# Attention scores in four query groups instead of two halves, PSUM as one tile, and padded TensorE steps

## The chip, the cores and the metric

The kernel runs on one core of a Trainium2 chip. The metric is the device time of one execution in microseconds (us). TensorE is called PE below, VectorE DVE, ScalarE ACT, GpSimd POOL, and SyncE, which issues most DMAs, SP.

## What is computed

One transformer layer with cross-attention, all in float32. `x` (queries) and `ctx` (keys and values) are 128 x 128 x 256: 128 sequences of 128 tokens. There are 16 heads of 16 channels and a hidden layer of 1024.

```
q = x @ Wq + bq ; k = ctx @ Wk + bk ; v = ctx @ Wv + bv        # 16 heads of 16
scores = q @ k^T / 4 ; keep only keys j < i ; attn = softmax(scores)
attn[row 0] = 0
y   = layer_norm(x + (attn @ v) @ Wo + bo, ln1)
out = layer_norm(y + relu(y @ W1 + b1) @ W2 + b2, ln2)
```

Query i sees only the keys before it. Half of each 128 x 128 score matrix is therefore never used.

## The kernel before

The kernel handles the sequences in pairs: 64 steps, one for each pair p. The order of instructions on every engine is written out by hand. The first steps (`third`, `fourth`, `fifth`, and what stands ahead of them) are special; from p = 5 on all are made by `step(p)`, and `behind` ends the pipeline. Several pairs are in work at the same time. `step(p)` issues in this order on PE:

- `weigh(p - 2)`: softmax weights times values into `pc` (PSUM bank 7), 96 matmul passes in 32-column strips of the array (L471, L481)
- `scores_both(p)`: the scores into `pss` (L364)
- `queries(p + 1)` into `pq` (bank 4), `attention_out(p - 2)` into `po` (bank 5), `keys(p + 1)` into `pk` (bank 0), `values(p)` into `pv` (bank 1)
- `second_by_seven(p - 4)`: the second FFN product into `py`, `pz` (banks 6 and 7, L780), as seven half-size products
- `hidden(p - 3)`: the first FFN product into `ph` (banks 2, 3, 4, 0, L687)

A float32 matmul shows up in the trace as two passes, each with a weight load (LDWEIGHTS, row PEld) and a MATMUL (row PE); a shape "32*64 32x128" means 32 rows by 64 columns of the array in use and 128 columns streamed. A transpose on PE is one pass.

The scores are made in two halves of queries. The low half (queries 0 to 63) gets 64 keys, the high half 128 keys. The two sequences of the pair sit in the two halves of the 128 partitions, and all 16 heads of a query lie in one partition. The high half goes to banks 0 to 3, one bank for each strip of four heads, the low half to banks 4 to 7. The array is used as 4 x 2 tiles of 32 rows and 64 columns: one row strip for each strip of heads, one column half for each sequence. `scores_both` alternates between the strips `two` and `one`, so that the banks that are needed soonest are read soonest.

DVE then adds the mask (`mask`, L378; `mask_high`, L729), takes maxima (L733, L740), ACT makes the exponentials head by head (`exponential_by_head`, L748), DVE sums them (`sums`, L409), POOL divides (L411), DVE transposes 32 x 32 blocks (`turn`, into `tb`, L424) and 16 DMAs on SP bring the blocks to the partitions of the keys (`bring`, into `pT`, L439). `weigh` uses `pT` two steps later. `sm`, `tb` and `pT` rotate through the four buffers of the pool tag `wide`. Each PSUM bank is a tile of its own (`at_bank`).

The first matmul of `pq` takes bank 4 and waits until DVE has read the low scores of that bank; that of `pk` takes bank 0 and waits for ACT; that of `pc` takes bank 7 and waits for `sum_of_seven` on DVE.

Of the kernel before, what the change touches and what calls it, by code (L numbers as in the profile page):

```python
# [13 lines left out]
P = 128  # L14
# [5 lines left out]
def tile_cross_attention_block(  # L20
# [53 lines left out]
    states = {}  # L74

# [96 lines left out]

    one = const.tile([1, P], F32, tag="one", name="one")
# [36 lines left out]
    def at_bank(i, name):  # L210
        return psum.tile([P, 512], F32, tag=f"b{i}", name=name)
# [101 lines left out]
    def wide(name):  # L313
        return soft.tile([P, NS * (H + HH) * 32], F32, tag="wide", name=name, bufs=4)
# [32 lines left out]
    def scores_both(p):  # L347

        st = states[p]
        for hi in range(2):  # L350
            st["sps", hi] = [
                at_bank(r if hi else (6, 7, 4, 5)[r], f"pss{hi}_{p}_{r}") for r in range(NS)
            ]
            room(p, hi)
        one, two = (0, 1), (2, 3)
        for strips, hi, m in (
            (two, 0, 0), (one, 1, 0), (two, 0, 1), (one, 1, 1),
            (two, 1, 0), (two, 1, 1), (one, 0, 0), (one, 0, 1),
        ):
            n = P if hi else HP  # L360
            for s in range(2):
                for r in strips:
                    strip, first = slice(32 * r, 32 * r + 32), s * P
                    nc.tensor.matmul(  # L364
                        st["sps", hi][r][
                            s * HP : (s + 1) * HP, m * 2 * n : (m + 1) * 2 * n
                        ].rearrange("p (e j) -> p e j", e=2),
                        st["qT"][strip, m, first + hi * HP : first + hi * HP + HP],
                        st["kT"][strip, m, :, first : first + n],
                        start=True, stop=True,  # L370
                    )

# [45 lines left out]
    def turn(p, hi, t):  # L418

        st = states[p]  # L420
        if "tb" not in st:
            st["tb"] = wide(f"tb_{p}").rearrange("p (j n) -> p j n", j=NS)
        at = (t if hi else 2) * 256
        nc.vector.transpose(  # L424
            st["tb"][:, :, at : at + 256].rearrange("p j (n a) -> p n j a", a=32),
            st["sm", hi].rearrange("p h j -> p (h j)")[:, t * 1024 : (t + 1) * 1024].rearrange(
                "p (n j a) -> p n j a", j=NS, a=32
            ),
        )

    def bring(p, queue, which):

        st = states[p]
        if "pT" not in st:
            pT = st["pT whole"] = wide(f"pT_{p}").rearrange("p (i n) -> p i n", i=NS)
            st["pT"] = pT.rearrange("p i (n a) -> p i n a", a=32)
        for u in which:
            i, j = u // NS, u % NS
            queue.dma_start(  # L439
                st["pT whole"][32 * j : 32 * j + 32, i, :], st["tb"][32 * i : 32 * i + 32, j, :]  # L440
            )

    def turn_on_pe(p, hi, ts):

        st = states[p]
        sm = st["sm", hi].rearrange("p h j -> p (h j)")
        if "pT" not in st:
            pT = wide(f"pT_{p}").rearrange("p (i n) -> p i n", i=NS)
            st["pT"] = pT.rearrange("p i (n a) -> p i n a", a=32)
        for t in ts:  # L450
            pt = bank(f"ptp{hi}_{p}_{t}")
            for i in range(4):
                at = (4 * t + i) * P
                nc.tensor.transpose(pt[:, i * P : (i + 1) * P], sm[:, at : at + P], ident)
            n = 4 * t if hi else H + 4 * t
            nc.scalar.copy(
                st["pT"][:, :, n : n + 4, :].rearrange("p i n a -> p n i a"),
                pt.rearrange("p (n i a) -> p n i a", i=NS, a=32),
            )

    def weigh(p):
# [3 lines left out]
        pc = at_bank(7, f"pc_{p}") if p > 1 else bank(f"pc_{p}")  # L465

        for m in range(KC):
            for s in range(2):
                at = (m * 2 + s) * P
                for j in range(NS):  # L470
# [3 lines left out]
                        pT[:, 2 * s : 2 * s + 2, H + 2 * j + m, :],  # L474
                        start=True, stop=True,
                    )
            for s in range(2):
                at = (m * 2 + s) * P
                for e in range(2):
                    for j in range(NS):  # L480
# [5 lines left out]
                            pT[:, 2 * s : 2 * s + 2, 4 * j + 2 * m + e, :],  # L486
# [189 lines left out]
    def hidden(p, fs, between=None):  # L676
# [3 lines left out]
        for f in fs[::2]:  # L680
# [4 lines left out]
            for i in range(2):  # L685
                for k in range(KC):
# [4 lines left out]
                    )  # L691
            for i in range(2):
# [31 lines left out]
    def mask_high(p, rs):  # L724

        st = states[p]
        for r in rs:
            ps = st["sps", 1][r].rearrange("p (n j) -> p n j", j=P)
            nc.vector.tensor_tensor(  # L729
                ps[:, :, HP:], ps[:, :, HP:], neg[:, 1, None, :].to_broadcast([P, 4, HP]), ALU.add  # L730
            )
        for r in rs:
            nc.vector.tensor_reduce(  # L733
                st["nmx", 1][:, 4 * r : 4 * r + 4],
                st["sps", 1][r].rearrange("p (n j) -> p n j", j=P), AX.X, ALU.max, negate=True,
            )

    def low_maximum(p):
        st = states[p]
        nc.vector.tensor_reduce(st["nmx", 0], st["sm", 0], AX.X, ALU.max, negate=True)  # L740

    def exponential_by_head(p, hi, heads):

        st = states[p]
        sm, nmx = st["sm", hi], st["nmx", hi]
        for h in heads:
            src = st["sps", 1][h // 4][:, h % 4 * P : h % 4 * P + P] if hi else sm[:, h, :]
            nc.scalar.activation(sm[:, h, :], src, AF.Exp, bias=nmx[:, h : h + 1], scale=1.0)  # L748
# [22 lines left out]
    def second_by_seven(p):  # L771
# [6 lines left out]
        def product(out, left, right):  # L778
            for k in range(FC // 2):
                nc.tensor.matmul(  # L780
                    out, left(k), right(k), start=(k == 0), stop=(k == FC // 2 - 1)
                )

# [6 lines left out]
        product(py[:, :P], raw(0, 0), weights(0, 0))  # L790
        product(pz[:, :P], raw(1, 0), weights(1, 0))
        product(pz[:, 2 * P : 3 * P], raw(1, 1), lambda k: wt[:, 3, k])
        product(py[:, 3 * P :], lambda k: hs[:, 0, k], lambda k: wt[:, 0, k])
        product(py[:, 2 * P : 3 * P], lambda k: hs[:, 2, k], lambda k: wt[:, 2, k])
        product(py[:, P : 2 * P], lambda k: hs[:, 1, k], lambda k: wt[:, 1, k])
        product(pz[:, P : 2 * P], lambda k: hs[:, 3, k], weights(1, 1))
# [159 lines left out]
    nc.gpsimd.tensor_tensor(be1b_r, be1_r, b2_r, ALU.add)  # L956
    values(2)
# [11 lines left out]
    def low_scores(p):  # L969
        scores(p, 0)  # L970
        mask(p, 0, A)
        mask(p, 0, B)
        maximum(p, 0, ALL)
# [3 lines left out]
    def third():  # L977
        p = 2
        scores(p, 1)
        mask(p, 1, A)  # L980
        maximum(p, 1, ONE)
# [5 lines left out]
        mask(p, 1, B)  # L987
        maximum(p, 1, TWO)
        exponential(p, 1, ONE)
# [7 lines left out]
        sums(p, 1, ONE)  # L997
        exponential(p, 1, TWO)
# [3 lines left out]
        exponential(p, 0, ALL)  # L1002
        sums(p, 1, TWO)
# [3 lines left out]
        sums(p, 0, ALL)  # L1007
        add_bo(2)
        turn(p, 1, 0)
        turn(p, 1, 1)  # L1010
        attention_out(p - 1)
        attention_sum(p - 1)
        turn(p, 0, 0)
        bring(p, nc.sync, EVERY[:8])
# [11 lines left out]
        hidden(0, range(3 * FC // 4, FC), lambda f: bring(p, nc.scalar, EVERY[8:]))  # L1026
# [3 lines left out]
    def fourth():  # L1030
        p = 3
        load_ahead(p)
        scores(p, 1)
        mask(p, 1, A)
        maximum(p, 1, ONE)
        second(0, 0)
        mask(p, 1, B)
        maximum(p, 1, TWO)
        exponential(p, 1, ONE)
        second(0, 1)  # L1040
        tokens(p + 2, "c")
        sums(p, 1, ONE)
        exponential(p, 1, TWO)
        second_sum(0)
        sums(p, 1, TWO)
        weigh(p - 1)
        context(p - 1)
        scores(p, 0)
# [3 lines left out]
        mask(p, 0, A)  # L1052
        mask(p, 0, B)
        maximum(p, 0, ALL)
        exponential(p, 0, ALL)
        turn(p, 1, 0)
        turn(p, 1, 1)
# [4 lines left out]
        sums(p, 0, ALL)  # L1062
# [4 lines left out]
        turn(p, 0, 0)  # L1067
        bring(p, nc.sync, LATE_FIRST)
        stats(0, states[0]["t2"], 2)
        scale_and_shift(0)  # L1070
        norm2(0)

    def fifth():
# [3 lines left out]
        mask(p, 0, B)  # L1077
        mask(p, 1, A)
        maximum(p, 1, ONE)
        queries(p + 1)  # L1080
        mask(p, 1, B)
        maximum(p, 1, TWO)
        exponential(p, 1, ONE)
        mask(p, 0, A)
        maximum(p, 0, ALL)
        keys(p + 1)
        exponential(p, 1, TWO)
        values(p)
        values_out(p)
        sums(p, 1, ONE)  # L1090
        exponential(p, 0, ALL)
        sums(p, 1, TWO)
        sums(p, 0, ALL)
# [5 lines left out]
        turn(p, 1, 0)  # L1099
        turn(p, 1, 1)  # L1100
        turn(p, 0, 0)
        bring(p, nc.sync, LATE_FIRST)
        hidden(2, range(FC // 2))

    ONES, TWOS = range(HH), range(HH, H)
    POOL_ALONE = (nc.gpsimd, nc.gpsimd)

    def step(p):
        last = p == NP - 1
        weigh(p - 2)  # L1110
        context(p - 2)
        scores_both(p)
        if p > 6:
            combine_hidden(p - 4, POOL_ALONE)
        if p == 5:
            second_sum(1)
            finish(0)
            store(0)
        add_bo(p - 1)
        load_ahead(p)  # L1120
        mask(p, 0, B)
        mask_high(p, A)
        exponential_by_head(p, 1, ONES)
        mask_high(p, B)
        exponential_by_head(p, 1, TWOS)
        mask(p, 0, A)
        low_maximum(p)
        if p > 5:
            exponential_by_head(p, 0, range(H))
# [9 lines left out]
        if p == 5:  # L1139
            exponential_by_head(p, 0, range(H))  # L1140
# [4 lines left out]
        sums(p, 1, ONE)  # L1145
        sums(p, 1, TWO)
        sums(p, 0, ALL)
# [12 lines left out]
        turn(p, 1, 0)  # L1160
        if p > 6:
            sum_of_seven(p - 4)
        turn(p, 1, 1)
        turn(p, 0, 0)
        bring(p, nc.sync, LATE_FIRST)
# [106 lines left out]
```

## Time and profile before

| what | value |
|---|---|
| time, median of 3 runs (lowest, highest) | 1553.75 us (1552.18, 1554.89) |
| the profiled execution: its time, its span | 1555.99 us, 1554.0 us |
| mean granted PE clock | 0.995 of full speed |
| busy: PE, DVE, POOL, ACT | 1521.2, 1327.8, 1265.7, 1120.5 us |
| passes on PE | 17926 |
| DMA moved | 204.21 MB, mean 131 GB/s |

The span runs from the first to the last instruction; the profiled execution takes 1.99 us more than its span and lies 2.24 us above the median. Ends of matmuls are modelled, so that starts are the better guide: the time of a stage is read from its first start to the first start of the stage after it.

### The profile page before, as it was taken

How to read it: one execution, taken by the hardware profiler on the slowest of the kernel's cores; microseconds unless marked ns; L12 is line 12 of the kernel's file. 1: busy time of each engine (PE TensorE's matmuls, PEld its weight loads, DVE VectorE, ACT ScalarE, POOL GpSimd, SP SyncE). 2: the span in 40 equal slices, each digit the busy share in tenths (PEclk: the TensorE clock that was granted, in tenths of full speed). 3: DMA queues.
4: the chain of work that ended last, by engine and by line, in shares of the span. 5: the costliest groups of instructions: out<-in, count | busy, mean ns of one | idle time of the engine just before them, and what ended most of it. 6: DMA issues, size and time to landing. Idle time of an engine off the chain costs nothing.

```text
span 1554.0 us, 47426 instructions
## 1 busy us (share of the span) xinstructions
PE 1521.2 (98%) x17926; PEld 1363.3 (88%) x17926; DVE 1327.8 (85%) x2490; ACT 1120.5 (72%) x3391; POOL 1265.7 (81%) x1290
## 2 busy tenths in 40 slices
PE   8997999999999999999999999999999999999998
PEld 7786989989899889899899899899898899899887
DVE  7987889888889889889889889889889889888854
ACT  5656778777778768778778778678778677777742
POOL 6875888887888888888888888888888888888874
PEclk9999999999999999999999999999999999999999
DMA  8355655555566556556556566556565566554431
GB/s 196 83 120 120 143 134 134 136 132 136 137 138 142 131 134 140 138 134 144 121 138 146 132 140 138 128 136 148 131 139 130 131 138 149 133 136 120 107 91 48
DMA packets 415283, 204.21 MB, mean 131 GB/s; under 512 B 282448, under 2 KB 383056, under 8 KB 415056
## 3 DMA queue, kind: packets, MB, share of 16 engines
q1 hardware_dynamic: 413152, 200.13, 55.7%
q8 instruction: 142, 2.33, 0.7%
q10 hardware_dynamic: 1904, 1.06, 0.3%
q14 instruction: 85, 0.70, 0.1%
HBM read 70.26 MB, written 33.29 MB: 67 GB/s over the span
## 4 chain that ended last, share of the span: by engine, by line
PE 92%; DVE 3%; POOL 3%; issue 1%; ACT 1%; DMA 0%; POOLq 0%; DVEq 0%
PE ph L687 27%; PE py L780 13%; PE pz L780 10%; PE pq L257 8%; PE po L500 7%; PE pv L289 7%; PE pk L257 7%; PE pss L364 6%; PE pc L481 3%; PE pc L471 2%; POOL sm L411 1%; PE py L705 0%; DVE tb L424 0%; DVE sm L378 0%; POOL sd L521 0%
## 5 line engine op out<-in xcount | busy, mean ns | idle before, releaser
L687 PE MATMUL ph<-x1T,w 128*128 128x256 f32 x2048 | 454.0, 379 | 3.0 <-ACT kT L279 3.0
L687 PEld LDWEIGHTS ph<-x1T,w 128*128 128x128 f32 x2048 | 384.6, 190 | 53.9 <-ACT kT L279 3.4
L411 POOL TENSOR_TENSOR sm<-sm,rs 128x1024 f32<-128x1024 f32 x192 | 359.3, 1898 | 7.1 <-ACT hT L693 4.5
L693 ACT ACTIVATE hT<-ph,b1e_c 128x256 f32<-128x256 f32 x504 | 209.8, 468 | 188.3 <-PE ph L687 181.3
L748 ACT ACTIVATE sm<-pss,nmx 128x128 f32<-128x128 f32 x944 | 249.8, 415 | 132.4 <-DVE nmx L733 72.5
L748 ACT ACTIVATE sm<-sm,nmx 128x64 f32<-128x64 f32 x944 | 231.9, 334 | 5.1
L409 DVE TENSOR_REDUCE su<-sm 128x8 f32<-128x1024 f32 (+1 forms) x192 | 225.8, 1176 | 9.4 <-ACT sm L748 5.6
L378 DVE TENSOR_TENSOR sm<-pss,neg 128x256 f32<-128x256 f32 (+1 forms) x276 | 108.0, 433 | 133.0 <-PE pss L364 125.2
L424 DVE STREAM_TRANSPOSE tb<-sm 128x1024 f32<-128x1024 f32 x186 | 220.7, 1213 | 0.0
L520 POOL TENSOR_SCALAR ve<-mv 128x2 f32<-128x2 f32 x127 | 29.7, 234 | 212.4 <-DVE mv L514 212.0
L780 PE MATMUL py<-wt,hS 128*128 128x128 f32 x1440 | 172.0, 276 | 2.9 <-POOL hS L767 2.9
L780 PEld LDWEIGHTS py<-wt,hS 128*128 128x128 f32 x1440 | 166.4, 192 | 3.5 <-POOL hS L767 3.5
L733 DVE TENSOR_REDUCE nmx<-pss 128x4 f32<-128x512 f32 x236 | 150.5, 678 | 0.0
L257 PE MATMUL pq<-xT,wq 128*128 128x256 f32 x504 | 127.3, 396 | 4.9 <-DVE sm L378 4.9
L279 ACT ACTIVATE kT<-pk,bkh,half 128x256 f32<-128x256 f32 x252 | 120.3, 558 | 4.0 <-PE pk L257 4.0
L289 PE MATMUL pv<-wv,cT 128*128 128x256 f32 x512 | 121.1, 379 | 1.6 <-ACT sm L748 1.6
L500 PE MATMUL po<-wo,cxT 128*128 128x256 f32 x512 | 122.4, 382 | 0.0
L257 PE MATMUL pk<-cT,wk 128*128 128x256 f32 x504 | 119.2, 379 | 0.0
L257 PEld LDWEIGHTS pq<-xT,wq 128*128 128x128 f32 x504 | 91.7, 192 | 25.8 <-issue 9.4
L289 PEld LDWEIGHTS pv<-wv,cT 128*128 128x128 f32 x512 | 97.1, 190 | 15.1 <-ACT sm L748 2.0
L500 PEld LDWEIGHTS po<-wo,cxT 128*128 128x128 f32 x512 | 98.0, 192 | 14.0 <-ACT cxT L493 0.3
L257 PEld LDWEIGHTS pk<-cT,wk 128*128 128x128 f32 x504 | 95.7, 190 | 13.1 <-issue 0.2
(131 smaller groups left out, 2973.3 us busy)
## 6 DMA issues: line engine op xcount, KB each, us to landing
pT<-tb SPq DMA_DIRECT2D x984, 96.0 KB
x1t<-tbx SPq DMA_DIRECT2D x252, 64.0 KB
x1T<-x1t SPq DMA_DIRECT2D x63, 256.0 KB
out_dram<-t SPq DMA_DIRECT2D x63, 256.0 KB
xb<-in_x_dram SPq DMA_DIRECT2D x124, 128.0 KB
cb<-in_ctx_dram SPq DMA_DIRECT2D x124, 128.0 KB
x<-in_x_dram SPq DMA_DIRECT2D x31, 512.0 KB
w<-in_L_xattn_W_dram SPq DMA_DIRECT2D x2, 1024.0 KB
```

Source lines behind the costliest of these rows:

```text
L257: nc.tensor.matmul(ps[:, m * TP : (m + 1) * TP], w[:, k, m * P : (m + 1) * P], src[:, k, :], start=(k == 0), stop=(k == KC - 1),)
L279: nc.scalar.activation(st["kT"][:, m, e, :], pk[:, m * TP : (m + 1) * TP], AF.Identity, bias=bkh[:, m, e : e + 1], scale=half[:, e : e + 1],)
L289: nc.tensor.matmul(pv[:, s * D : (s + 1) * D], st["cT"][:, k, s * P : (s + 1) * P], wv[:, k, :], start=(k == 0), stop=(k == KC - 1),)
L409: nc.vector.tensor_reduce(su, sm[:, part, :], AX.X, ALU.add)
L411: nc.gpsimd.tensor_tensor(sm[:, part, :], sm[:, part, :], rs[:, :, None].to_broadcast([P, part.stop - part.start, n]), ALU.mult,)
L424: nc.vector.transpose(st["tb"][:, :, at : at + 256].rearrange("p j (n a) -> p n j a", a=32), st["sm", hi].rearrange("p h j -> p (h j)")[:, ...
L500: nc.tensor.matmul(po[:, s * D : (s + 1) * D], cxT[:, k, s, :], wo[:, k, :], start=(k == 0), stop=(k == KC - 1),)
L687: nc.tensor.matmul(ph[:, i * TP : (i + 1) * TP].rearrange("p (s i a) -> p s i a", s=2, a=32), w1[:, k, (f + i) * P : (f + i + 1) * P], st[ ...
L693: nc.scalar.activation(st["hT"][:, f + i, :], ph[:, i * TP : (i + 1) * TP], AF.Relu, bias=(b1e_c if p else b1_c)[:, f + i : f + i + 1], sc ...
L733: nc.vector.tensor_reduce(st["nmx", 1][:, 4 * r : 4 * r + 4], st["sps", 1][r].rearrange("p (n j) -> p n j", j=P), AX.X, ALU.max, negate=True,)
L748: nc.scalar.activation(sm[:, h, :], src, AF.Exp, bias=nmx[:, h : h + 1], scale=1.0)
L780: nc.tensor.matmul(out, left(k), right(k), start=(k == 0), stop=(k == FC // 2 - 1))
```

## The change

Scores, softmax and the way to `pT` work in four groups g of 32 queries, with 32, 64, 96 and 128 keys. A partition now holds a query of one sequence for one half of the heads: 2 sequences x 2 head halves x 32 queries make the 128 partitions, with 8 heads in each. The array is used as 4 x 4 tiles of 32 x 32 (row strip of heads, column strip c of sequence and head half). A step has 64 score matmuls (128 passes) in place of 32 (64 passes).

- All of PSUM is one tile `banks`, and `at_bank` returns a slice of it. Groups 3 and 2 share banks 0 to 3, groups 1 and 0 banks 4 to 7.
- `sm`, `nmx`, `su`, `rs` hold four groups; a partition has 2560 weights in place of 3072. `wide` has two buffers: `sm` always takes one and `tb` the other. `pT` is two constant tiles, zeroed once by `clear` where no DMA writes. The 16 DMAs stay, two of four shapes shorter.
- The masks of the last 32 keys of each group come from one 128 x 128 tile `diag`; `mask_high` adds them for groups 3 and 2 in one instruction for two banks.
- `empty(n)` issues n empty instructions (`nop`) on PE: 10 or 11 after each of the seven products of `second_by_seven`, and 3 or 4 after each matmul of `hidden` for p < 3.
- At p = 5, `second_sum(1)` stands before the scores.

The core of the diff:

```diff
+    banks = psum.tile([P, 8, 512], F32, tag="banks", name="banks")
     def at_bank(i, name):
-        return psum.tile([P, 512], F32, tag=f"b{i}", name=name)
+        return banks[:, i, :]
+
+    def empty(n):
+        for _ in range(n):
+            nc.tensor.nop(hint="pad", nofuse=True)
...
+    LENGTH = (32, 64, 96, 128)
+    WITHIN = (0, 32, 0, 96)
+    HI, LO = (3, 2), (1, 0)
+    def first_bank(p, g):
+        return 4 if p > 3 and g < 2 else 0
+    def place(g, r):
+        return r if g > 1 else (r + 2) % 4
...
+    def group_scores(p, g, strips=range(NS)):
+        st = states[p]
+        n = LENGTH[g]
+        for m in range(KC):
             for s in range(2):
+                c = 2 * s + m
                 for r in strips:
                     strip, first = slice(32 * r, 32 * r + 32), s * P
+                    out = banks[32 * c : 32 * c + 32, first_bank(p, g) + place(g, r)]
                     nc.tensor.matmul(
...
-                        st["qT"][strip, m, first + hi * HP : first + hi * HP + HP],
+                        out.rearrange("p (e x) -> p e x", e=2)[:, :, WITHIN[g] : WITHIN[g] + n],
+                        st["qT"][strip, m, first + 32 * g : first + 32 * g + 32],
                         st["kT"][strip, m, :, first : first + n],
                         start=True, stop=True,
                     )
+    def scores_both(p):
+        one, two = (0, 1), (2, 3)
+        for strips, g in (
+            (two, 1), (one, 3), (two, 0), (one, 2),
+            (two, 3), (one, 1), (two, 2), (one, 0),
+        ):
+            group_scores(p, g, strips)
...
+    def masked(p, g, at=slice(0, 4)):
+        n = LENGTH[g]
+        heads = slice(2 * at.start, 2 * at.stop)
+        nc.vector.tensor_tensor(
+            weights(p, g)[:, heads], in_banks(p, g, at),
+            diag[:, None, P - n :].to_broadcast([P, 2 * (at.stop - at.start), n]), ALU.add,
+        )
...
-        def product(out, left, right):
+        def product(out, left, right, after):
             for k in range(FC // 2):
                 nc.tensor.matmul(
                     out, left(k), right(k), start=(k == 0), stop=(k == FC // 2 - 1)
                 )
+                empty(after // (FC // 2) + (after % (FC // 2) > k))
...
     def step(p):
...
-        mask(p, 0, B)
-        mask_high(p, A)
-        exponential_by_head(p, 1, ONES)
-        mask_high(p, B)
-        exponential_by_head(p, 1, TWOS)
-        mask(p, 0, A)
-        low_maximum(p)
+        for g in LO:
+            masked(p, g, FORE)
+        mask_high(p, FORE)
+        exponential_by_head(p, HI, ONES)
+        mask_high(p, REAR)
+        exponential_by_head(p, HI, TWOS)
+        for g in LO:
+            masked(p, g, REAR)
+        for g in LO:
+            largest(p, g)
```

`FORE` and `REAR` are the first and the last two banks of a group of four. The order of the other calls in `step` is as before.

More of the change, by code (lines that the diff above doesn't have):

```diff
@@ L345, in scores @@
         room(p, hi)
-    def scores_both(p):
-        st = states[p]
[L350 to L360, printed above, removed]
+    pTs = []
@@ L373, in mask, with brought @@
+    def brought(p, queue, which):
+        st = states[p]
+        st["pT"] = pTs[p % 2]
+        pT = pTs[p % 2].rearrange("p i t n a -> p i (t n a)")
+        for u in which:
+            i, j = u // NS, u % NS
+            first = (0, 128, 0, 384)[j]
+            queue.dma_start(
+                pT[32 * j : 32 * j + 32, i, first:], st["tb"][32 * i : 32 * i + 32, j, first:]
+            )
     def mask(p, hi, rs):
@@ L978, in third @@
         p = 2
-        scores(p, 1)
-        mask(p, 1, A)
-        maximum(p, 1, ONE)
+        for g in HI:
+            group_scores(p, g)
+        masked(p, 3)
+        shifted(p, 3)
         turn_x1_on_pe(0)
@@ L1051, in fourth @@
         queries(p + 1)
[L1052 to L1057, printed above, removed]
+        for g in LO:
+            masked(p, g)
+        for g in LO:
+            shifted(p, g)
+        for g in LO:
+            powers(p, g)
+        turned(p, 3)
+        turned(p, 2)
         attention_out(p - 1)
@@ L1066, in fourth @@
         turn_x1(p - 1)
[L1067 to L1068 removed]
+        for g in LO:
+            turned(p, g)
+        brought(p, nc.sync, LATE_FIRST)
         stats(0, states[0]["t2"], 2)
```

284 lines of the change are left out of this document (173 added, 111 removed).

## The prediction

> **What bounds the kernel now.** I read the page's busy times and its chain first, then the table by stretches for one step in the middle, then the timeline of PE for that step, and last PE's idle times.
>
> ```profile
> PE 1521.2 (98%) x17926; PEld 1363.3 (88%) x17926; DVE 1327.8 (85%) x2490; ACT 1120.5 (72%) x3391; POOL 1265.7 (81%) x1290
> 319.56:342.85 23.29, 23.29 (x281) 21.07 (x280) 20.65 (x40) 17.74 (x55) 19.63 (x20) 1.00 0.56 125
> 342.85:367.85 25.00, 23.67 (x281) 21.20 (x280) 20.85 (x40) 17.85 (x55) 20.87 (x24) 1.00 0.62 146
> ```
>
> The second and third rows are two steps that follow each other, each from the start of its `weigh` to the next one's: length, then busy time of PE, PEld, DVE, ACT and POOL, the granted clock, DMA. In the first PE is busy all 23.29 us, at full clock, and DVE is the next with 20.65. So in a plain step only what PE itself does counts. The second step is 1.71 us longer, and PE is idle for 1.33 us in it. How a plain step is made up, from the timeline of PE (start, length, line, count):
>
> ```profile
> 812.74 0.43 PE L471 MATMUL pc<-pT,vd 128*32 128x64 f32 x16
> 814.22 1.63 PE L364 MATMUL pss<-kT,qT 32*64 32x128 f32 x64
> 815.78 1.99 PE L257 MATMUL pq<-xT,wq 128*128 128x256 f32 x8
> 817.61 1.89 PE L500 MATMUL po<-wo,cxT 128*128 128x256 f32 x8
> 822.79 1.05 PE L780 MATMUL py<-w,hT 128*128 128x128 f32 x8
> 823.68 1.06 PE L780 MATMUL pz<-w,hT 128*128 128x128 f32 x8
> 829.04 7.07 PE L687 MATMUL ph<-x1T,w 128*128 128x256 f32 x32
> 836.04 0.43 PE L471 MATMUL pc<-pT,vd 128*32 128x64 f32 x16
> ```
>
> From start to start: `weigh` 1.48, scores 1.56, and every other pass at the rate of its columns: eight passes of 128 columns in 0.89 (111 ns each), 32 of 256 in 7.00 (219, the drain included). The 96 passes of `pc`, in four column strips side by side, take 15.4 ns each, so 62 ns for each strip's pass of 64 columns. A pass thus costs some 0.82 ns a column and 6 ns; TensorE streams without a break.
>
> The third piece is what makes some steps longer. The weight loads of the scores that found nothing to do:
>
> ```profile
> 129.90 0.42 PEld L364 LDWEIGHTS pss<-kT,qT 32*64 32x64 f32 x21 [1.22 <-issue]
> 347.23 0.19 PEld L364 LDWEIGHTS pss<-kT,qT 32*64 32x64 f32 x3 [1.58 <-issue]
> 557.85 0.19 PEld L364 LDWEIGHTS pss<-kT,qT 32*64 32x64 f32 x3 [0.87 <-issue]
> 768.82 0.19 PEld L364 LDWEIGHTS pss<-kT,qT 32*64 32x64 f32 x4 [1.16 <-issue]
> 979.17 0.19 PEld L364 LDWEIGHTS pss<-kT,qT 32*64 32x64 f32 x4 [0.58 <-issue]
> 1190.08 0.20 PEld L364 LDWEIGHTS pss<-kT,qT 32*64 32x64 f32 x5 [1.19 <-issue]
> 1400.42 0.20 PEld L364 LDWEIGHTS pss<-kT,qT 32*64 32x64 f32 x5 [0.61 <-issue]
> q8 instruction: 142, 2.33, 0.7%
> ```
>
> "issue" means that PE waited for nothing that the profile shows. From the second row on they come every 210.6 us, nine steps. The last row is the queue that brings PE's instructions: 142 packets of 16.4 KB, one for some 256 of the 36,400 instructions. A step of the built program has 569 PE instructions; nine make 5121, 20 blocks and 1 instruction over, so every ninth step lies alike to the blocks. Counted in the trace, all seven stalls fall on number 193 of a block. So PE waits for its own instructions: `weigh` and the scores issue 320 in 3 us, a block change falls 57 behind the start of `weigh`, and the next, 256 on, comes before its block is there. The six stalls behind the first sum to 5.99 us; the step shown lost 0.13 more than its idle row, so the six cost 6.8 us.
>
> **The sum, part by part.**
>
> *Place of the blocks.* With the empty instructions the changed program has exactly 768 PE instructions, three blocks, from one `weigh` to the next, from step 7 to the end of `step`. `weigh` always starts on number 225, and the scores end 450 later. Changes lie 32 ahead of `weigh`, 224 behind its start (in the scores) and 480 behind it (in `po`). The first is passed in `hidden`, long before. The second is passed some 1.7 us into the stretch, and its follower is needed at 1.48 + 1.56 + 1.83 (`pq`) + seven passes of `po` (1.5) = 6.4 us, 4.7 us later. In the stalled step the change was passed at about 0.4 us and PE went on at 347.23 - 342.85 = 4.4 us, so a block takes up to 4.0. The margin is 0.7 us, and a stall there would be small. Value: -6.8; between -6.8 and -3.
>
> The Trainium skill ("Runtime: NRT & Kernel Launch", Instruction fetch mechanics) states blocks of 16 KiB or 256 instructions, as here, and that crossing a block is mostly hidden; by that this term would be nothing and the time 1552.5. The stalls above, 0.58 to 1.58 us, speak against it in this stretch.
>
> *The empty instructions themselves.* 74 in a step of `second_by_seven`. The trace has none; the nearest thing that only PE's sequencer handles is a wait:
>
> ```profile
> L364 PEldq EVENT_SEMAPHORE  x119: 51/51/51, 84.5 to 1468.9; - x119
> ```
>
> A half-size matmul streams for 2 x 111 = 223 ns and has 2.6 of them behind it: 2.6 x 51 = 135 ns of issue. They hide behind the stream, and `hidden` behind them (64 instructions in 7 us) gives the lead back. The three or four behind each matmul of the first three `hidden` have 2 x 216 ns and hide too. The cover is gone above 84 ns each. If they held the array they would cost 74 x 51 ns = 3.8 us a step. Value 0.
>
> *The scores on PE.* 128 passes in place of 64, but on 16 tiles in place of 8. For one tile, before: four passes of 128 columns and four of 256, 4 x 111 + 4 x 216 = 1.31 us of the 1.56; the other 0.25 are filling and draining. After: two passes each of 64, 128, 192 and 256, 2 x (58 + 111 + 163 + 216) = 1.10, so 1.35 us. That needs passes of all tiles side by side. The trace shows eight so:
>
> ```profile
> 814.22 0.49 PE L364 MATMUL pss<-kT,qT 32*64 32x128 f32 x12
> 815.04 0.76 DVE L378 TENSOR_TENSOR sm<-pss,neg 128x256 f32<-128x256 f32 x2 [2.13 <-PE pss L364]
> ```
>
> The first row is all that began from 814.22 to 814.45: 12 passes in 0.23 us, each of which streams 0.11 to 0.22. The `pc` passes show four column strips at once. If strips `two` and `one` wait for each other in program order, group 3 of `two` begins only when group 3 of `one` has ended: 432 + 432 + 326 ns (groups 3, 3, 2) = 1.19, so 1.44 us. There is also a new floor: the first `pq` pass takes bank 4 and now waits for two DVE instructions, groups 1 and 0. DVE began 0.82 behind the first score pass; the two groups are done 2 x (111 + 58) = 338 ns on in place of 444, so it begins at about 0.72, and 0.41 + 0.31 (below) bring it to 1.44, with the way back to PE 1.5. So a step saves 0.06 at best. A second weight load that is not hidden, or a queue too short for 32 instructions between two uses of a tile, costs some 0.1. Over 58 steps: between -3.5 and +6; I take 0, in the middle and nearest to the row of the scores now.
>
> *DVE, POOL, ACT, DMA.* In a plain step nothing, since they are covered by PE. DVE's masks and maxima, from the groups (busy, mean ns of one):
>
> ```profile
> L378 DVE TENSOR_TENSOR sm<-pss,neg 128x256 f32<-128x256 f32 x256 | 95.4, 414 | 132.2 <-PE pss L364 125.2 <-DMA pT<-tb 5.1 <-PE pss L336 1.5
> L729 DVE TENSOR_TENSOR pss<-pss,neg 128x256 f32<-128x256 f32 x236 | 89.0, 422 | 0.0
> L733 DVE TENSOR_REDUCE nmx<-pss 128x4 f32<-128x512 f32 x236 | 150.5, 678 | 0.0
> L740 DVE TENSOR_REDUCE nmx<-sm 128x16 f32<-128x1024 f32 x59 | 72.0, 1220 | 2.1
> L808 DVE TENSOR_TENSOR t<-x1b,py 128x512 f32<-128x512 f32 x60 | 39.1, 651 | 7.6 <-PE py L780 5.2 <-DMA out_dram<-t 2.4
> ```
>
> Before: 4 x 414 + 4 x 422 + 4 x 678 + 1220 = 7.3 us. From 414 at 256 elements and 651 at 512, an add of 128 takes some 0.3; from 678 and 1220, a maximum of 384 some 0.55, of 256 some 0.42. After: 2 x (0.41 + 0.3) + 2 x (0.42 + 0.68 + 0.55) + 0.68 + 0.42 = 5.8. One new wait: `tb` has one buffer, so DVE's first `turned` waits for the 16 copies of the step before.
>
> ```profile
> 835.78 11.80 SPq L439 DMA_DIRECT2D pT<-tb  x15
> 852.23 1.20 DVE L424 STREAM_TRANSPOSE tb<-sm 128x1024 f32<-128x1024 f32 x1
> ```
>
> The copies are issued by 847.6 and the transpose starts at 852.2. DVE comes up to 2.5 us earlier, so 2 us stay for landing. If that is short, `sum_of_seven`, behind it on DVE, is late, and `pc` waits for that at 859; DVE has 2.13 us of idle to give.
>
> *The first steps.* There PE does wait:
>
> ```profile
> 119.39 1.99 PE L687 MATMUL ph<-x1T,w 128*128 128x256 f32 x8 [3.01 <-ACT kT L279]
> 124.87 1.99 PE L825 MATMUL py<-w,hT 128*128 128x256 f32 x8 [1.75 <-ACT hT L693]
> 136.10 3.78 PE L257 MATMUL pq<-xT,wq 128*128 128x256 f32 x8 [4.91 <-DVE sm L378]
> ```
>
> The chain runs through p = 5: masks and maxima, `attention_sum`, statistics, POOL, ACT. It gets the 1.5 us shorter that DVE saves, and loses some 0.2 for more instructions: -1.3, between -4 and +2, since the order of the first steps changes too. Step 5 and 6 still cross a block in the scores, in the shade of these waits.
>
> *Sum.* -6.8 + 0 + 0 - 1.3 = -8.1. The profiled span of 1554.0 becomes 1545.9, its execution 1547.9; that execution is 2.24 us above the median of 1553.75, so the median becomes 1545.6.
>
> **The rivals.**
>
> *Passes are paid by number.* If small tiles don't overlap as I take it, a pass costs at least what one of `pc` costs: 128 x 15.4 = 1.97 us, +0.41 a step, +24 over 58 steps: 1553.75 - 8.1 + 24 = 1570. At the rate of the scores now (24.4 ns) it is 3.12 us, +91, 1636. For it: 128 passes of 32 x 32 occur nowhere in the trace. Against it: the 12 starts in 0.23 us, 19 ns each and in bursts. It decides from 15 ns a pass. Chance 0.15 (0.12 and 0.03). The Trainium skill ("TensorE: Matmul & The Clock Gate", "Wait — 56ns, not 53.3ns?") says that starts are never closer than about 25 ns; by that the scores would take 3.2 us and the kernel 1641. The 15.4 ns of `pc` disagree.
>
> *Stalls go, scores grow.* The queue on PE is too short for the longer way between two uses of a tile: +0.1 to +0.14 a step, +6 to +8, which takes back the gain: 1552 to 1554. For it: program order puts 64 instructions there where there were 32. Chance 0.14.
>
> *The blocks are reached too soon in every step, or the empty instructions hold PE.* A stall of 0.6 to 1.6 in all 58 steps gives about +64, so near 1610; 3.8 us a step gives 1766. Against: the margin of 0.7 us, the 135 of 223 ns. Chance 0.09.
>
> **How the numbers follow.** The forecast has 0.62, with a range of its own from 1539 to 1551. No run of this kernel can tell less than about 0.2% (3.1 us) from no change: faster is below 1550.6, slower above 1556.9. Faster 0.62; same is the second rival, 0.14; slower the two others, 0.24. The range goes from 1539 (below it 0.04) to 1572, which takes in the passes at 15.4 ns and leaves out 0.12 above.
>
> **What would show it.** Right: every step from the seventh within 0.1 us of 23.29, no "issue" row in the scores, 1.45 to 1.6 us from the first score pass to `pq`, 111 ns for each half-size pass. Wrong: scores of 1.9 us or more, "issue" idle in each step, or `py` and `pz` stages longer than 0.89.

## The result, and the profile after

| | median us (lowest to highest) | runs |
|---|---|---|
| before | 1553.83 (1552.18 to 1554.89) | 4 |
| after | 1575.03 (1573.26 to 1575.19) | 4 |

The ratio is 1.0133, 95% interval 1.0121 to 1.0145: the change costs 21 us where 8 were to be gained. The time lies above the range of the prediction, which ended at 1572.

First the busy times of the page of after and the queue that brings PE's instructions, then one plain step (from one `weigh` to the next; columns as in the prediction):

```profile
PE 1545.9 (98%) x21894; PEld 1385.6 (88%) x21894; DVE 1208.4 (77%) x2548; ACT 1089.3 (69%) x3394; POOL 1226.3 (78%) x1364
q8 instruction: 190, 3.11, 0.9%
797.29:821.05 23.76, 23.76 (x346) 21.49 (x345) 18.70 (x40) 17.24 (x55) 18.96 (x22) 1.00 0.51 112
```

DVE did get lighter (1327.8 to 1208.4 us busy), POOL too, and PE's queue brings 190 packets of instructions where it brought 142. PE, busy all through, now takes 23.76 us a step where it took 23.29. The timeline of PE for that step says in which stage (start, length, line, count):

```profile
797.29 0.43 PE L572 MATMUL banks<-pT,vd 128*32 128x64 f32 x16
798.78 2.07 PE L412 MATMUL banks<-kT,qT 32*32 32x128 f32 x128
800.78 1.99 PE L271 MATMUL banks<-xT,wq 128*128 128x256 f32 x8
802.61 1.89 PE L603 MATMUL banks<-wo,cxT 128*128 128x256 f32 x8
807.79 1.95 PE L881 MATMUL banks<-w,hT 128*128 128x128 f32 x16
814.04 6.21 PE L790 MATMUL banks<-x1T,w 128*128 128x256 f32 x28
```

From start to start, as the median of the 56 plain steps of each trace: `weigh` 1.493 us (1.478 before), scores 2.003 (1.549), `pq` 1.831 (the same), `second_by_seven` 6.251 (the same, although 74 empty instructions now lie in it), `hidden` 7.002 (the same). So 0.454 of the 0.469 us are in the scores.

The sum closes. The first plain `weigh` (step 7) starts 0.84 us earlier than before; 56 plain steps at 0.469 give +26.3; the stalls, 6.8 us before, are 0.2 now, -6.6; what follows the last plain step takes 1.2 us less. That is +17.7, and the profiled spans differ by 1571.5 - 1554.0 = 17.5. The medians differ by 3.7 more: the profiled run of after was the shortest of its four (the others had spans of 1573.2 to 1573.5), that of before was longer than its median.

Inside the scores, the passes and the weight loads that are in work in a stretch (the counts in brackets), after and then before:

```profile
798.78:798.90 0.12, 0.12 (x16) 0.12 (x30) 1.00 0.00 0
799.22:799.34 0.12, 0.12 (x30) 0.12 (x14) 1.00 1.07 230
```

```profile
814.22:814.34 0.12, 0.12 (x8) 0.12 (x15) 1.00 0.05 0
814.70:814.82 0.12, 0.12 (x22) 0.12 (x12) 1.00 0.33 102
```

A matmul has two weight loads and two passes. In the first 0.12 us of after 16 matmuls begin, as many as there are tiles, 6.7 ns apart. The 17th starts at 0.32 us. From the 18th on, 0.43 us behind the first, they follow at 16.7 ns (14 loads, so 7 matmuls, in 0.12 us), and between such runs no weight load begins for 0.1 to 0.2 us at a time. Before, with 32 matmuls, this is covered by the chain of one tile, 1.31 us (short_before, below).

### The profile page after: what moved, and what is told of

Its sections match the earlier page's. It is cut to its first block, busy times and chain, and to the rows that moved or that the text cites. A ratio compares the mean times of both kernels' runs of the same rounds, so it can differ in the third digit from the quotient of the medians.

```text
span 1571.5 us, 59475 instructions
## 1 busy us (share of the span) xinstructions
PE 1545.9 (98%) x21894; PEld 1385.6 (88%) x21894; DVE 1208.4 (77%) x2548; ACT 1089.3 (69%) x3394; POOL 1226.3 (78%) x1364
## 4 chain that ended last, share of the span: by engine, by line
PE 94%; POOL 2%; DVE 2%; ACT 1%; DMA 1%; issue 1%; SPq 0%; ACTq 0%; POOLq 0%; DVEq 0%
PE banks L790 27%; PE banks L881 23%; PE banks L271 14%; PE banks L412 7%; PE banks L603 7%; PE banks L303 7%; PE banks L583 3%; PE banks L572 2%; PE banks L810 0%; ACT sm L847 0%; POOL sm L537 0%; DMA pT<-tb 0%; DMA c_first<-in_ctx_dram 0%; DMA x1T<-x1t 0%; PE banks L1346 0%
## 5 line engine op out<-in xcount | busy, mean ns | idle before, releaser
L790 PE MATMUL banks<-x1T,w 128*128 128x256 f32 x2048 | 453.9, 379 | 2.0 <-ACT kT L293 1.2
L790 PEld LDWEIGHTS banks<-x1T,w 128*128 128x128 f32 x2048 | 384.4, 190 | 53.0 <-ACT kT L293 1.6
L798 ACT ACTIVATE hT<-banks,b1e_c 128x256 f32<-128x256 f32 x504 | 211.2, 471 | 222.5 <-PE banks L790 222.3
L847 ACT ACTIVATE sm<-banks,nmx 128x128 f32<-128x128 f32 (+1 forms) x944 | 237.0, 402 | 154.4 <-POOL hS L869 141.8
L847 ACT ACTIVATE sm<-sm,nmx 128x64 f32<-128x64 f32 (+1 forms) x944 | 223.0, 422 | 0.0
L460 DVE TENSOR_REDUCE su<-sm 128x8 f32<-128x1024 f32 x248 | 192.3, 796 | 30.0 <-ACT sm L847 24.3
L881 PE MATMUL banks<-wt,hS 128*128 128x128 f32 x1440 | 171.4, 275 | 2.2 <-POOL hS L868 2.2
L881 PEld LDWEIGHTS banks<-wt,hS 128*128 128x128 f32 x1440 | 165.9, 192 | 2.7 <-POOL hS L868 2.6
L439 DVE TENSOR_REDUCE nmx<-banks 128x4 f32<-128x512 f32 x236 | 136.3, 620 | 4.0
L412 PE MATMUL banks<-kT,qT 32*32 32x64 f32 (+3 forms) x7936 | 130.9, 305 | 2.3 <-issue 1.7
```

The lines of the kernel that those rows point to most:

```text
L412: nc.tensor.matmul(out.rearrange("p (e x) -> p e x", e=2)[:, :, WITHIN[g] : WITHIN[g] + n], st["qT"][strip, m, first + 32 * g : first + 32 ...
L439: nc.vector.tensor_reduce(states[p]["nmx"][:, g, heads], src, AX.X, ALU.max, negate=True)
L460: nc.vector.tensor_reduce(su[:, g], weights(p, g), AX.X, ALU.add)
L790: nc.tensor.matmul(ph[:, i * TP : (i + 1) * TP].rearrange("p (s i a) -> p s i a", s=2, a=32), w1[:, k, (f + i) * P : (f + i + 1) * P], st[ ...
L798: nc.scalar.activation(st["hT"][:, f + i, :], ph[:, i * TP : (i + 1) * TP], AF.Relu, bias=(b1e_c if p else b1_c)[:, f + i : f + i + 1], sc ...
L847: nc.scalar.activation(sm[:, h], src, AF.Exp, bias=st["nmx"][:, g, h : h + 1], scale=1.0)
```

## The experiments

Four theories stood against each other for the scores: *number* (how many matmuls), *small tiles* (32x32), *streams* (the lengths of the groups), *order* (a matmul whose tile is busy holds those behind it). For the empty instructions it was *place* against *their own cost*. All times are medians; ratios are to the kernel before, run on the same chip.

This table has, for one middle step of each kernel, counted in its trace: score matmuls and tiles, what a tile streams by the durations of the prediction, the start of the last score pass behind the first, and the stage up to `pq`.

| kernel | matmuls, tiles | a tile's streams | last start | stage |
|---|---|---|---|---|
| before | 32 on 8 | 1.31 us | 1.354 | 1.549 |
| short_before | 32 on 8 | 0.46 | 1.055 | 1.200 |
| half_passes | 32 on 8 | 1.10 | 1.140 | 1.542 |
| after | 64 on 16 | 1.10 | 1.824 | 2.003 |
| short_streams | 64 on 16 | 0.46 | 1.397 | 1.534 |
| equal_pairs | 64 on 16 | 1.10 | 1.903 | 2.765 |
| two_then_one | 64 on 16 | 1.10 | 2.226 | 2.369 |
| split_before | 64 on 8 | 1.35 | 2.130 | 2.275 |
| split_far | 64 on 8 | 1.35 | 1.681 | 1.877 |

**The count without the small tiles (split_before, split_far).** The kernel before with each score matmul cut in two:

```
-for s, r: matmul(..., kT[strip, m, :, first : first + n])      # 32 a step
+for e, s, r: matmul(..., kT[strip, m, e, first : first + n])   # 64 a step
```

> The kernel before with each of its 32 score matmuls cut in two by the key half, so 64 matmuls and 128 passes a step as after the change, but on 8 tiles of 32x64 and all of one kind (eight passes of 64 columns and eight of 128 for a tile); the result is the same. Empty instructions make the step 768 instructions with weigh on number 225, as after the change. Theory 'number' (the count of score instructions sets the stage): scores 1.95 to 2.05 us, a plain step 23.7 to 23.8, and 1553.8 - 6.8 + 58 x 0.45 = 1573. Theory 'small tiles' (the price is that of 32x32 tiles) and theory 'streams' (unequal lengths and the order of the groups): 8 x 58 + 8 x 111 ns = 1.35 us for a tile, with 0.25 for filling and draining 1.60, a plain step 23.35 and 1553.8 - 6.8 + 3 = 1550.

Measured: 1592.0 us, ratio 1.0237 (1.0223 to 1.0251).

```profile
808.96 2.35 PE L370 MATMUL pss<-kT,qT 32*64 32x64 f32 x128
811.24 1.99 PE L261 MATMUL pq<-xT,wq 128*128 128x256 f32 x8
```

The scores take 2.28 us on the old tiles, with the old softmax: more than after the change. So it does not take small tiles: the number, or the order that came with it, is enough. But 2.275 is above the 1.95 to 2.05 that the number alone was to give. What differs is that the two halves of a matmul, for the same tile, lie only four matmuls apart. split_far puts them eight apart:

> The kernel before with its score matmuls cut in two as in split_before (64 matmuls on 8 tiles of 32x64, 768 instructions a step), in another order: the second half of a matmul comes 8 matmuls behind the first and not 4, and the strips alternate to the end. Theory 'number and waits' (16 matmuls 6.7 ns apart, each further one 16.7 ns, 107 + 48 x 16.7 = 0.91 us, and waits where a tile is wanted again too soon): the waits shrink with the longer way, the scores fall from 2.275 to 1.8 to 2.1 us, 1562 to 1582. Theory 'a fixed price for a matmul of this kind': 2.25 to 2.30 us, 1589 to 1593.

Measured: 1570.8 us, ratio 1.0102 (1.0078 to 1.0127); the scores fall to 1.88 us. The same 64 matmuls on the same tiles differ by 0.40 us through their order alone; there is no fixed price for a matmul. And against the kernel before, with the same 8 tiles, 1.35 us of streams for 1.31 and a tile wanted again after 8 matmuls (4 to 12 there), the doubled number costs 0.33 us: the number counts by itself.

```profile
798.97 1.95 PE L373 MATMUL pss<-kT,qT 32*64 32x64 f32 x128
800.85 1.99 PE L261 MATMUL pq<-xT,wq 128*128 128x256 f32 x8
```

**Half the count on small tiles (half_passes).** After, without the matmuls of m = 1 (the `m` loop of `group_scores` runs over this last argument), so half of the heads' scores are left out:

```
-group_scores(p, g, strips)
+group_scores(p, g, strips, range(1))     # scores from step 5 on
```

> The changed kernel from step 5 on without the score matmuls of m = 1: half of the heads' scores are left out, 32 matmuls on 8 of the 16 tiles, 32x32 as before, each tile with the same passes as in the change. A step then has 640 instructions. Theory 'number': 128 instructions as in the kernel before, so scores of 1.3 to 1.55 us and 1575 - 58 x 0.45 to 0.7 = 1534 to 1549. Theory 'small tiles': each matmul keeps its price, so scores of 1.0 to 1.2 us (pq's wait for DVE is the floor) and 1575 - 58 x 0.8 to 1.0 = 1517 to 1529. Theory 'streams': the chain of every tile that is left is the same, so scores stay at 1.9 to 2.0 us and 1570 to 1575.

Measured: 1546.4 us, ratio 0.9946 (0.9931 to 0.9961). The last pass starts at 1.14 us in place of 1.82, with the same chain on each tile that is left. *Streams* (1.9 to 2.0) is out. The stage, 1.54, lies where *number* put it, but this run does not decide against *small tiles*, which split_far does: the stage ends there since `pq` then waits for DVE, and inside it a weight load at 0.80 us waits for ACT, which reads bank 7 until 0.75.

```profile
809.07 1.19 PEld L412 LDWEIGHTS banks<-kT,qT 32*32 32x32 f32 x64
810.61 0.51 PEld L271 LDWEIGHTS banks<-xT,wq 128*128 128x128 f32 x3 [0.35 <-DVE sm L432]
```

This is the floor of 1.5 us that the prediction worked out (1.44 and the way back to PE).

**Shorter streams (short_streams, short_before).** All scores on 32 keys, in after and in before; the scores of the other keys are left out. short_before also has 8 empty instructions a step, to keep the place of the blocks, and PSUM as one tile:

```
-n = LENGTH[g]                                  # short_streams
+n = LENGTH[g] if p < 4 else 32
...
-st["kT"][strip, m, :, first : first + n],      # short_before
+st["kT"][strip, m, :, first : first + 32],
```

> The changed kernel from step 4 on with all four groups of scores on 32 keys: the scores of the keys beyond are left out; number, tiles and order of the matmuls stay. A tile's chain falls from 1.10 us to 8 x 58 ns = 0.46. Theory 'number' and theory 'small tiles': scores stay at 1.8 to 2.0 us, 1563 to 1575. Theory 'streams': scores fall to 0.8 to 1.1 us, with pq's wait for DVE as the floor, 1575 - 58 x 0.9 to 1.2 = 1505 to 1523.

> The kernel before, placed as before_576, with PSUM as one tile, and with every score matmul of step 5 and later on 32 keys: the scores of the keys beyond are left out. 32 matmuls on 8 tiles; a tile's chain falls from 1.31 us to 8 x 58 ns = 0.46. The last score pass now starts 1.354 us behind the first. Theory 'number and waits': 107 + 16 x 16.7 = 0.37 us and waits for weights of 0.1 to 0.4, so it starts at 0.45 to 0.8 us, and the scores before were bound by their streams where those after are not (1.397 us with streams as short). Theory 'a fixed price for each matmul': 1.2 to 1.35 us. The time by the first: pq's wait for DVE becomes the floor at 1.1 to 1.3 us, 1547.8 - 58 x 0.25 to 0.45 = 1522 to 1533; by the second 1540 to 1548.

Measured: 1550.7 us (ratio 0.9977, 0.9967 to 0.9986) and 1530.3 us (0.9841, 0.9818 to 0.9865). Neither theory of the first was right: the stage takes 1.53 us and the last pass starts at 1.40, between the two forecasts. With streams of 0.46 us a tile, 64 matmuls still need 1.40 us, so most of the stage after the change isn't a tile's streaming. At 16.7 ns without a break they would need 107 + 48 x 16.7 ns = 0.91 us; the rest, 0.49 here and 0.43 more with the longer streams of after, are holds. The second missed its place (1.055 us for 0.45 to 0.8) through a wait that I had not priced: the 26th matmul is the first on bank 7, which ACT reads until 0.76 us behind the first score pass, and it begins at 0.82 with the six others behind it.

```profile
802.13 0.58 ACT L498 COPY cxT<-banks 128x508 f32<-128x508 f32 x1 [0.71 <-ACT hT L700]
801.95 1.13 PEld L369 LDWEIGHTS banks<-kT,qT 32*64 32x64 f32 x64
```

The 25 matmuls ahead of it had all begun by 0.61 us, in the forecast range.

**The order on small tiles (equal_pairs, two_then_one).** After, with the groups issued in another order:

```
-(two, 1), (one, 3), (two, 0), (one, 2), (two, 3), (one, 1), (two, 2), (one, 0)
+(two, 3), (one, 3), (two, 2), (one, 2), (two, 1), (one, 1), (two, 0), (one, 0)   # equal_pairs
+(two, 1), (two, 0), (two, 3), (two, 2), (one, 3), (one, 2), (one, 1), (one, 0)   # two_then_one
```

> The changed kernel with the same score matmuls in another order: group 3 on both pairs of strips, then 2, 1, 0, so that what alternates is of equal length; pq then waits longer for DVE, so the stage is read from its first to its last pass start (1.825 us now). Theory 'in order': a matmul whose tile is busy holds all behind it; pairs then take 432 + 326 + 222 + 216 ns in place of 432 + 326 + 432 + 326, and the last pass starts at 1.45 to 1.65 us. Theory 'number alone': the last pass starts at 1.80 to 1.85 us. The time by either: pq waits 0.7 us behind the scores, 1575 + 58 x 0.2 to 0.5 = 1587 to 1604.

> The changed kernel with the same score matmuls in another order: all four groups of strips 2 and 3 first, then all of strips 0 and 1, so a tile is used again after 8 matmuls and not after 16. Theory 'in order': the tiles of the second half stand idle behind the first half, each half takes at least its chain of 1.10 us, and the scores take 2.4 to 2.9 us, 1598 to 1627. Theory 'number alone': 1.95 to 2.05 us, 1572 to 1578.

Measured: 1618.5 us (1.0403, 1.0386 to 1.0420) and 1594.4 us (1.0246, 1.0229 to 1.0263). Both theories missed both times. Equal lengths side by side did not shorten the passes (last start 1.903, not 1.45 to 1.65, nor quite the 1.80 to 1.85 of *number alone*); `pq` then waits for DVE, so the order of the change is the better one:

```profile
796.43 2.11 PE L412 MATMUL banks<-kT,qT 32*32 32x256 f32 x128
799.20 1.99 PE L271 MATMUL banks<-xT,wq 128*128 128x256 f32 x8 [0.65 <-DVE sm L432]
```

Keeping to half of the tiles costs 0.37 us (2.369), just under the 2.4 to 2.9 of *in order* and far above *number alone*. What after, equal_pairs and short_streams have in common is this: 16 matmuls begin in one go; the 18th loads its weights much later (in after at 0.433 us, in equal_pairs at 0.645, in short_streams at 0.326); from there one follows every 16.7 ns, with further holds. It is not the busy tile of the 17th that holds them: in two_then_one the 18th loads its weights at 0.432 us and the 17th's second pass starts at 0.570. It goes with the first matmul. In all nine kernels of the table the 18th loads its weights 0.187 to 0.189 us after the first one's second pass has streamed (its start plus its stream, by the durations of the prediction: after 0.133 + 0.111, equal_pairs 0.240 + 0.216, short_streams 0.080 + 0.058, two_then_one 0.134 + 0.111, split_far 0.107 + 0.058 with the load at 0.354, before 0.160 + 0.111 with the load at 0.459). 16 matmuls are 64 instructions. The Trainium skill ("TensorE: Matmul & The Clock Gate", the table at its head and Part 3) gives TensorE a queue of 64 with limited reordering, which agrees with the 16 x 4 seen here. Its sentence that matmuls start and end strictly in program order doesn't: the second pass of the first matmul starts 0.133 us in, behind the first pass of the 16th at 0.109.

The long holds behind the 18th matmul of after follow the same rule, 17 places on. The 26th, the 42nd and the 43rd load their weights at 0.699, 1.090 and 1.240 us; the second passes of the 9th, the 25th and the 26th start at 0.293, 0.738 and 0.888, and with their streams (0.216, 0.163, 0.163) and 0.188 that gives 0.697, 1.089 and 1.239. So, as these traces read, 17 matmuls are in work at most, and one more comes in when the one 17 places ahead is done. Cutting a matmul in two halves what these 17 stream, and the order decides how soon the one 17 places ahead is done. In after all holds sum to 1.824 - 0.107 - 48 x 0.0167 = 0.92 us, the last matmul's own second pass (some 0.08) included; the short ones among them (20 to 60 ns) were not worked out.

**The place of the blocks (before_576, no_empty, place_97).** First the kernel before, with 7 empty instructions a step, 44 in the first steps to set the place, and nothing else:

```
 for k in range(FC // 2):
     nc.tensor.matmul(out, left(k), right(k), ...)
+    empty(after // (FC // 2) + (after % (FC // 2) > k))      # after = 1 for each of the seven
```

> The kernel before with 7 empty instructions a step, one behind the first matmul of each of the seven products, so 576 instructions, and 44 more in the first steps, which place weigh on numbers 40, 104, 168 and 232 of a block in turn, away from 134 to 139 where the stalls came. Nothing else is changed. Theory 'place of the blocks' (term 1 of the prediction): the six stalls go and nothing comes, 1553.8 - 6.8 = 1547. Rival 'stalls come anyway' (with the place only their moment changes): 1551 to 1555, with an issue row in the scores every few steps.

Measured: 1547.8 us, ratio 0.9949 (0.9936 to 0.9962), five runs. Every plain step takes 23.29 us; none stalls:

```profile
807.44:830.73 23.29, 23.29 (x282) 21.07 (x281) 20.66 (x40) 17.73 (x55) 19.65 (x20) 1.00 0.64 149
830.73:854.02 23.29, 23.29 (x282) 21.07 (x281) 20.65 (x40) 17.74 (x55) 19.63 (x20) 1.00 0.56 126
```

This version beats both kernels. Now the changed kernel without its empty instructions (`empty` returns at once), and with 128 fewer of them ahead of the plain steps:

> The changed kernel without its empty instructions: 694 PE instructions a step, so the place of weigh in a block moves by 74 places back from step to step. Theory 'place of the blocks': the stages keep their lengths (scores 2.00, second_by_seven 6.25), and stalls of 0.5 to 1.6 us come back in the steps whose change of block falls badly; weigh and the scores are 448 instructions now, so at least as many as in the kernel before: 1575 + 6 to 15 = 1581 to 1590. Theory 'empty instructions cost time': second_by_seven becomes shorter than 6.25 us by up to 0.1, 1569 to 1575. If neither, 1575.

> The changed kernel with 128 fewer empty instructions in the first steps, so that weigh starts on number 97 of a block in every step and not on 225; nothing else is changed, the step stays at 768 instructions. Theory 'place of the blocks': the neighbours of that place in the kernel without empty instructions lost 1.62 us (95) and 1.81 us (101) a step in the scores; 56 steps x 1.6 to 1.8 = 90 to 101, 1665 to 1676. Rival 'it is the period of 768, not the place, that lets the fetch run ahead': 1575.

Measured: 1632.7 us (1.0489, 1.0458 to 1.0520) and 1708.3 us (1.1001, 1.0967 to 1.1034). Weight loads of the scores that waited for nothing the profile shows: sum in us, times, longest; in after (all five ahead of the plain steps), without the empty instructions, and at place 97:

```profile
PEld banks L412 <- issue: 3.5, 5, 1.6
```

```profile
PEld banks L411 <- issue: 52.4, 40, 2.1
```

```profile
PEld banks L412 <- issue: 106.2, 60, 2.4
```

Apart from `pq` and `po`, the other stages kept their lengths. Without the empty instructions the 56 plain steps lie at 56 places. In 20 of them `weigh` starts between numbers 153 and 243: these lost 0.03 us each, none more than 0.14. The 36 others lost 0.6 to 2.2 us each, but for one with 3.6, 54.7 together, nearly all of the 57.7 by which this kernel is slower than after. I had expected 6 to 15. In the kernel before, with 320 instructions in `weigh` and the scores in place of 448, six plain steps were hit. At place 97 each step lost 1.3 us or more, as the neighbours 95 and 101 had shown (1.6 and 1.8); but 17 of 56 lost over 3 us. In these 17 plain steps, and in no other, the granted clock is 0.5 for 3.41 us behind the stall, and `pq` and `po` together take 1.0 to 1.7 us longer. (The step with 3.6 us above has such a stretch too, worth 1.7.) The stretch in the first plain step, columns as before:

```profile
162.27:165.69 3.42, 3.42 (x11) 2.80 (x9) 3.00 (x7) 3.20 (x14) 2.48 (x2) 0.50 0.42 100
```

Without these 27 us the 56 plain steps lost 96.5, within the 90 to 101 forecast from single steps; the forecast had left out the clock. The weight loads of the scores in one step there, from the timeline:

```profile
940.73 1.09 PEld L412 LDWEIGHTS banks<-kT,qT 32*32 32x32 f32 x80
943.62 0.67 PEld L412 LDWEIGHTS banks<-kT,qT 32*32 32x32 f32 x48 [1.80 <-issue]
```

The stop comes behind 80 loads, 192 + 160 = 352 instructions behind the start of `weigh`, and 97 + 352 = 256 + 193: number 193 of a block, the number at which the stalls of the kernel before had come. So the rival 'the period, not the place' is out: with the same 768 instructions a step, the place is worth 1708 - 1575 = 133 us, the clock's share included. The Trainium skill ("Runtime: NRT & Kernel Launch", Instruction fetch mechanics) calls the crossing of a block mostly hidden; it is at 20 places of 56 here.

**Empty instructions by themselves (nops_in_scores).** The kernel before with two behind each score matmul, and 19 or 20 behind the matmuls of each of the seven products:

```
 nc.tensor.matmul(...)      # scores
+empty(2)
```

> The kernel before with two empty instructions behind each of its 32 score matmuls, 64 in all, and 135 behind the products of second_by_seven: 768 instructions a step, weigh on number 225 as after the change. The scores still are 64 passes on 8 tiles. Theory 'instructions of any kind are supplied at 4.2 ns each' (16.7 ns for the four of a matmul): scores 1.55 + 64 x 4.2 ns = 1.8 us at most, 1547 + 58 x 0.1 to 0.27 = 1553 to 1563. Theory 'it is matmuls alone': scores 1.55 us, 1547. Theory 'an empty instruction costs what a wait costs' (51 ns): 3.3 us more, 1738.

Measured: 1871.0 us, ratio 1.2017 (1.1990 to 1.2044). The scores take 5.61 us:

```profile
799.21 5.67 PE L368 MATMUL pss<-kT,qT 32*64 32x128 f32 x64
804.82 1.99 PE L261 MATMUL pq<-xT,wq 128*128 128x256 f32 x8
```

All three theories missed. Matmuls now follow each other at 161 ns, so an empty instruction costs (161 - 17) / 2 = 72 ns where nothing hides it: neither 4.2 nor 51. A product of `second_by_seven` has four half-size matmuls of 223 ns each. In after two or three empty instructions follow each, on average 2.64 x 72 + 17 = 207 ns: they are hidden (6.251 us). Here four or five follow, some 364 ns: the first 19 of the 28 matmuls still come every 223 ns, those behind mostly 374 ns apart where five stand between, (374 - 17) / 5 = 71 ns for each, and the stage grows to 7.54 us. So the 16.7 ns of a score matmul are its own, not a rate for instructions of any kind.

## Why the prediction was wrong

*Place of the blocks* (-6.8): right. The stalls of the plain steps went from 6.8 to 0.2 us. before_576 shows the same term alone at -6.3. The term was understood too small, though: in the changed program the empty instructions and their place are worth 58 us (no_empty), presumably since its dense stretch has 448 instructions and not 320; no run changes that alone.

*Empty instructions* (0): right; no stage that holds them became longer. The cost taken (51 ns, from a wait) was too low; at 72 ns the 2.64 behind a half-size matmul still hide behind its 223 ns, with 16 ns to spare, which is why it did not matter.

*Scores on PE* (0, between -3.5 and +6): this is the step that failed. It measured 56 x 0.454 = +25.4 us. The sum took the stage for the chain of one tile, 1.10 us, filling and draining included 1.35. The support for it, that 12 passes started in 0.23 us, was the burst of matmuls at the head of the stage; I read it as the rate for all. With 32 matmuls in the kernel before the chain (1.31 us) hides everything else. With 64, four on each of 16 tiles, the chain is the shorter part: short_streams cuts it to 0.46, and the last pass still starts at 1.40 us. What the sum left out is that a matmul also waits for the one 17 places ahead of it, on whatever tile that one is. The trace of before had no 64 matmuls on small tiles to show this; for an operation not shown, the nearest price of another stage, 15.4 ns a pass and +24 us in all, belonged into the bounds of this term, and I had put it into a rival and let the term end at +6.

*Rival 1, passes paid by number* (1570, 0.12): nearest to the time, and half right in its mechanism. The number counts by itself (split_far), and small tiles are not needed for it; but 15.4 ns a pass was a price from another stage, and there is no fixed price: 64 matmuls took 1.40 to 2.23 us to their last start, by streams and order. That 128 x 15.4 ns = 1.97 lies near 2.00 is no proof of it. *Rival 2* (a queue too short for the longer way between two uses) was nearest to the mechanism of the holds, and too small in size, 0.10 to 0.14 for 0.45. *Rival 3* did not happen at place 225, and does at 97.

*DVE, POOL, ACT, DMA* (0) and *the first steps* (-1.3, -4 to +2): right. DVE lost 119 us of busy time, and PE's plain step shows none of it; that `weigh` became 0.015 us longer, 0.8 in all, was in no term. The first plain step began 0.84 us earlier; the end gave another 1.2 that the sum did not have.

## What to carry to other kernels

A burst shows what a queue held, not what it can sustain: before a pass is cut into twice as many, look for the longest run of such passes, and where the bursts end. Here 17 matmuls were in work at a time, whatever their size; smaller ones give those 17 less to stream. When an engine stands still for nothing that the profile shows, count its instructions to the next block; a few empty instructions behind long streams can move the change of block out of the densest stretch, and a change that makes the stretch denser needs that more. Take such a placing and a change of the work as two edits and time each alone: here the one was worth -6 us, the other +26.

## What the runs showed of the hardware

- Score matmuls (four instructions each) on 16 tiles of 32x32 begin 6.7 ns apart up to the 16th; from the 18th on they follow at 16.7 ns at best, on tiles of 32x64 too. The 18th loads its weights 0.19 us after the first has streamed its second pass, in nine kernels; in after the long holds behind it come 17 places on in the same way.
- Cutting 32 matmuls on 8 tiles into 64 of half the stream cost 0.33 or 0.73 us a stage, depending on the order alone.
- An empty instruction on TensorE costs 72 ns unhidden; two or three (2.64 on average) hide behind a matmul of 223 ns, four or five (4.8) don't.
- With 448 instructions in 3.5 us, a change of block costs 0.6 to 2.2 us at 36 of 56 places; with 320 in 3 us, it cost 0.7 to 1.7 us at one step in nine.
- At place 97, 17 of 56 stalled steps also had 3.41 us of granted clock 0.5, worth 27 us in all.
